# Layer 3 of a four-layer cross-attention kernel: a written plan of rounds for an item's four stages

## The chip, the core and the metric

The kernel runs on one core of a Trainium2 chip. The metric is the device time of one execution in microseconds (us); the time given for a kernel is the median of its runs. A profiled execution is a separate run, taken by the hardware profiler, with its own time.

## What is computed

The reference applies four transformer layers one after the other to `x` of 8 items of 256 tokens by 320 channels, in float32, with a context of 120 tokens by 192 channels per item. Layers 0 and 1 have self-attention, cross-attention and a gated feed-forward part, and layer 2 has cross-attention to the text and to the image tokens. The change is in layer 3, which has 8 heads of 40 channels:

```python
query = hidden_states @ Wq
keyt, valt = enc @ Wk, enc @ Wv                          # 116 context tokens
hs = _mha(query, keyt, valt)                             # 256 queries on 116 keys
ca_q1 = einsum('btc,th->bch', ca, Wq_ca)[:, indices, :]  # 192 distinct queries from 4 tokens
ca_hs1 = _mha(ca_q1, residual, residual)                 # 192 queries on the item's 256 tokens
ca_q2 = ca_hs1 @ Wq
ca_hs2 = _mha(ca_q2, ca @ Wk_ca, ca @ Wv_ca)             # on 4 keys
out = (hs + ca_hs2) @ Wout + b_out + residual
```

`_mha` is softmax attention. A softmax needs each query's largest score first, so every score is computed twice here: once to find the largest, once (with the largest already subtracted through an added row of the operands) for the exponential.

## The kernel before

TensorE multiplies into PSUM, which is cut into three double banks (`self.pair()`, tiles `pf`) and two single banks (`self.bank()`, tiles `pa`). A matmul that opens a new tile has to wait until the last reader of an earlier tile in that place is done. VectorE (DVE) finds maxima, takes reciprocals and normalises; ScalarE (ACT) takes exponentials and copies; GpSimd (POOL) adds the bias row; SyncE (SP) issues the DMAs.

`run_flow` goes over a list of 40 items; the last eight, one per batch entry, are layer 3's, built by `last_item`. Each item has four stages, written as generators, and each `yield` ends a step. In round `step` four generators are open together: the largest scores of the next item (`tops`), the projections of the item after that (`project`), the output product of the item before (`fin`), and the attention of the item itself (`out`). Before the change they advance in turn, one step each per turn, in that order, until all are empty. The Tile framework then sets each engine's fixed order of instructions from the order of emission, its priorities and its own estimates; on the chip every engine keeps to that order and waits on semaphores.

The steps of layer 3, with short names used in the rest of the text and the lines of the kernel before:

- **P1** transposes of the item (L339), loads of `cs`, `kz`, `v`, masks `bd` (L985). **P2** queries (lwq, L132 and L139). **P3** `z` and `u` (wz, L132, L139, L1009).
- **T1** largest scores of the queries: two halves of 16 matmul records (L1027), each with one maximum `negm` on DVE (L1031). **T2**, **T3** largest scores of the further attention (L1041, 16 records in two double banks), each with two maxima `negc` (L1046). **T4** transposes of these maxima (L1054, L1057), a copy to `nT` on ACT (L1061), and six small DMAs of `nT` into `cs` and `qT` (L1063, L1065).
- **O1** the further scores, first half, and exponentials (`further(0)`, L1077, L1083). **O2** nothing. **O3** `further(1)` and `further_values(0)` (L1109, reciprocal L1115, `oc` L1116). **O4** `context(0)` (L1092, exponential L1098) and `further_values(1)`. **O5** `context(2)`, the small softmax (product with `m` at L120, then `mx`, `p`, `sm`), `context_values(0)`. **O6** `context_values(1)` and `(2)`. **O7** `context_values(3)`, the product with `sel`, `pT`, `xb`. Each `context_values` is 16 records (L1123) into one single bank, a reciprocal `rs` (L1129) and a product `oT` (L1130) on DVE, which frees the bank.
- **F1**, **F2** one output product each (L120, 8 records with `lwo` and 2 with `v2W`), the addition to `x_sb` (L1185) and the store.

Of the kernel before, what the change touches and what calls it, by code (L numbers as in the profile page):

```python
# [54 lines left out]
class Kernel:  # L55
# [619 lines left out]
    def run_flow(self, items, before={}, after={}):  # L675


        n = len(items)
        made = {}
        for step in range(-2, n + 1):  # L680
            if step + 2 < n:
                if step + 2 in before:
                    before[step + 2]()
                made[step + 2] = items[step + 2]()
            order = ((step + 1, 1), (step + 2, 0), (step - 1, 3), (step, 2))
            gens = [made[i][k]() for i, k in order if 0 <= i < n]
            while gens:
                for g in list(gens):
                    try:
                        next(g)  # L690
                    except StopIteration:
                        gens.remove(g)
            if step in after:
                after[step]()

# [254 lines left out]
    def last_item(self, b, w, brow, to):  # L950
# [66 lines left out]
        def tops():  # L1017
            qT, kT, z, cs = it["q"], it["k"], it["z"], it["c"]
            negm = self.small.tile([P, 2, G3, TPB], F32, tag="negm", name="negm3")
            negc = self.small.tile([P, 4, 2, 2], F32, tag="negc", name="negc")  # L1020
            for g0 in range(0, G3, 2):
                s = self.pair()
                for i in range(2):
                    for t in range(TPB):
                        for j in range(2):
                            r, o = j * PAD3, (i * TPB + t) * K3
                            nc.tensor.matmul(  # L1027
                                s[:, j, o : o + K3], qT[r : r + PAD3, g0 + i, t * P : (t + 1) * P],
                                kT[r : r + PAD3, g0 + i, :], start=True, stop=True,
                            )  # L1030
                nc.vector.tensor_reduce(  # L1031
                    negm[:, :, g0 : g0 + 2, :].rearrange("p j g t -> p j (g t)"),
                    s[:, :, : 4 * K3].rearrange("p j (t k) -> p j t k", k=K3), AX.X, ALU.max, negate=True,
                )
            yield
            for g in range(2):
                s = [self.pair() for _ in range(2)]
                for t in range(2):
                    for j in range(4):
                        r = j * PAD  # L1040
                        nc.tensor.matmul(  # L1041
                            s[j // 2][:Q3, j % 2, t * N : (t + 1) * N], cs[r : r + PAD, g, t * Q3 : (t + 1) * Q3],
                            z[r : r + PAD, g, :], start=True, stop=True,
                        )
                for i in range(2):
                    nc.vector.tensor_reduce(  # L1046
                        negc[:Q3, 2 * i : 2 * i + 2, g, :], s[i][:Q3].rearrange("p j (t k) -> p j t k", k=N),
                        AX.X, ALU.max, negate=True,
                    )
                yield  # L1050
            nT = self.work.tile([8, 2 * N], F32, tag="nT", name="nT3", bufs=1)
            ps = self.bank()
            for t in range(2):
                nc.tensor.transpose(  # L1054
                    ps[:8, t * P : (t + 1) * P], negm.rearrange("p j g t -> p (j g) t")[:, :, t], self.ident
                )
                nc.tensor.transpose(  # L1057
                    ps[:8, N + t * Q3 : N + (t + 1) * Q3], negc[:Q3].rearrange("p j g t -> p (j g) t")[:, :, t],
                    self.ident[:Q3, :Q3],
                )  # L1060
            nc.scalar.copy(nT[:, : N + CC], ps[:8, : N + CC])  # L1061
            for g in range(2):
                nc.sync.dma_start(cs[T3::PAD, g, :], nT[g::2, N : N + CC])  # L1063
            for g in range(G3):
                nc.sync.dma_start(qT[D3::PAD3, g, :], nT[g::G3, :N])  # L1065
# [111 lines left out]
        def fin():  # L1177
            x, xb, (oT, pT) = self.x[:, TPB * b : TPB * (b + 1), :], it["xb"], it["out"]
            r = b * HT % P
            for t in range(TPB):  # L1180
# [5 lines left out]
                nc.sync.dma_start(to[b, o, :], x[:, t])  # L1186
                yield

        return project, tops, out, fin


class Quant:
# [630 lines left out]
```

## Time and profile before

| what | value |
|---|---|
| median of 3 runs | 2202.73 us (2201.51 to 2212.49) |
| profiled execution, its own time | 2203.86 us |
| its span, first to last instruction | 2202.1 us |
| TensorE (PE) busy | 2036.4 us, 92% of the span |
| VectorE (DVE) busy | 1112.6 us, 51% |
| ScalarE (ACT) busy | 833.3 us, 38% |
| layer 3's items, output product to output product | 34.92 us (2007.27 to 2042.19) |
| in such a stretch (2007 to 2042): PE, DVE, ACT busy | 33.54, 19.92, 9.62 us |

Line names such as L1129 are lines of the kernel before. A row of the timeline gives start, busy time, engine, line, operation and operands, a count, and the idle time ahead of it with what ended it. A busy PE row includes pipelined matmuls whose ends are modelled, so the start-to-start distance of two groups is the better cost of a group.

### The profile page before, as it was taken

Reading aid. Unit: us, or ns where it says so; the run is one execution under the profiler, and the core shown is the slowest. Engines: PE = TensorE matmul, PEld = TensorE weight load, DVE = VectorE, ACT = ScalarE, POOL = GpSimd, SP = SyncE. Lnnn points to the kernel's source line nnn. Section 1 sums busy time; section 2 is a strip of 40 time slices with the busy share of each in tenths; the row PEclk is TensorE's granted clock in tenths of the full one; section 3 lists DMA queues with packets and bytes.
Section 4 is the critical chain, followed back from the end, with each engine's and each line's share of the span. In section 5 each row is a group of like instructions: output and inputs, shape, how many; then the busy total and the mean of one; then the engine's idle time right before and its main releaser. Section 6 shows DMA issues by size and latency. Waiting matters only on the chain.

```text
span 2202.1 us, 38254 instructions
## 1 busy us (share of the span) xinstructions
PE 2036.4 (92%) x16415; PEld 1194.6 (54%) x16415; DVE 1112.6 (51%) x1698; ACT 833.3 (38%) x1259; POOL 330.5 (15%) x358
## 2 busy tenths in 40 slices
PE   7888889898889999999999998899999999999997
PEld 5643345554444465465555555544555655666664
DVE  5388687445651222235555567621121666546565
ACT  3456888367542121124444444311201333222221
POOL 3194033723010000000000010100000100000100
PEclk9989889898899999999999999999999999999999
DMA  4000000642120000020000101100000120000000
GB/s 118 20 12 2 2 1 1 174 111 57 52 85 14 1 0 1 1 93 2 2 2 22 28 25 36 47 1 0 1 0 1 24 68 23 19 16 26 23 19 16
DMA packets 79303, 63.21 MB, mean 29 GB/s; under 512 B 48410, under 2 KB 68318, under 8 KB 78622
## 3 DMA queue, kind: packets, MB, share of 16 engines
q1 hardware_dynamic: 75070, 57.06, 9.4%
q10 hardware_dynamic: 4064, 3.71, 0.6%
q8 instruction: 129, 2.11, 0.4%
q14 instruction: 40, 0.33, 0.0%
HBM read 42.61 MB, written 17.37 MB: 27 GB/s over the span
## 4 chain that ended last, share of the span: by engine, by line
PE 73%; DVE 15%; issue 4%; ACT 4%; POOL 2%; DMA 2%; SPq 0%; ACTq 0%; DVEq 0%; POOLq 0%
PE pf L594 13%; PE pf L120 11%; PE pf L132 9%; PE pa L120 7%; PE pa L456 6%; PE pf L439 4%; PE pa L594 3%; PE pf L139 3%; DVE negm L1456 3%; PE pf L394 3%; PE pf L736 3%; DVE rs L464 3%; PE pf L1497 2%; PE pa L1519 2%; DVE negm L401 2%
## 5 line engine op out<-in xcount | busy, mean ns | idle before, releaser
L445 ACT ACTIVATE e<-pf 128x1024 f32<-128x1024 f32 (+2 forms) x176 | 158.5, 946 | 220.1 <-PE pf L439 213.1
L401 DVE TENSOR_REDUCE negm<-pf 128x4 f32<-128x1024 f32 (+4 forms) x224 | 188.1, 887 | 97.9 <-PE pf L394 97.9
L594 PE MATMUL pf<-xTf,ff 128*128 128x512 f32 x512 | 230.8, 597 | 6.2 <-DVE negm L401 5.2
L464 DVE RECIPROCAL rs<-pa 128x256 f32<-128x256 f32 x88 | 152.3, 1745 | 143.5 <-PE pa L456 143.5
L1504 ACT ACTIVATE e<-pf,sc_s 128x1024 f32<-128x1024 f32 x160 | 169.8, 1118 | 48.7 <-PE pf L1497 44.8
L1456 DVE TENSOR_REDUCE negm<-pf 128x4 f32<-128x1024 f32 (+2 forms) x128 | 143.3, 1151 | 69.6 <-PE pf L1453 58.2
L619 DVE SCALAR_TENSOR_TENSOR hT<-pf,cols_sb,gl 128x512 f32<-128x512 f32 x64 | 48.0, 751 | 256.4 <-ACT gl L618 254.1
L120 PE MATMUL pf<-ff,hT 128*128 128x320 f32 x640 | 174.4, 434 | 0.0
L594 PEld LDWEIGHTS pf<-xTf,ff 128*128 128x128 f32 x512 | 94.3, 190 | 125.4 <-issue 118.5
L120 PEld LDWEIGHTS pf<-ff,hT 128*128 128x128 f32 x640 | 120.9, 190 | 55.5 <-issue 6.1
L618 ACT ACTIVATE gl<-pf,cols_sb 128x512 f32<-128x512 f32 x64 | 44.0, 689 | 247.8 <-PE pf L594 247.8
L439 PE MATMUL pf<-qT,kT 32*128 32x256 f32 (+1 forms) x1280 | 122.1, 410 | 9.1 <-DVE negm L401 7.5
L394 PE MATMUL pf<-kT,qT 32*128 32x120 f32 (+1 forms) x1920 | 113.1, 326 | 18.6 <-ACT e L445 18.3
L487 POOL TENSOR_TENSOR xb<-x_sb,brow 128x640 f32<-128x640 f32 x24 | 37.0, 1543 | 563.8 <-DVE x_sb L493 555.4
L120 PE MATMUL pa<-o,oT 128*128 128x320 f32 x352 | 105.7, 441 | 15.2 <-DVE oT L465 15.2
L394 PEld LDWEIGHTS pf<-kT,qT 32*128 32x128 f32 x1920 | 83.0, 186 | 58.4 <-ACT e L445 27.5
L647 POOL TENSOR_TENSOR xb<-x_sb,brow 128x640 f32<-128x640 f32 x16 | 25.0, 1563 | 573.8 <-DVE x_sb L652 528.2
L1497 PE MATMUL pf<-Q,K 32*128 32x256 bf16 (+1 forms) x960 | 90.5, 295 | 21.7 <-DVE negm L1456 11.5
L456 PE MATMUL pa<-e,v 128*32 128x256 f32 (+1 forms) x1280 | 106.1, 391 | 2.3 <-ACT e L445 1.7
L1606 DVE TENSOR_SCALAR w<-e 128x1024 bf16<-128x1024 f32 (+2 forms) x128 | 89.2, 703 | 32.3 <-ACT e L1504 31.1
L132 PE MATMUL pf<-xT,q 128*128 128x256 f32 x384 | 100.5, 391 | 0.4 <-ACT e L445 0.2
L439 PEld LDWEIGHTS pf<-qT,kT 32*128 32x128 f32 (+1 forms) x1280 | 68.4, 182 | 55.5 <-DVE negm L401 26.9
(291 smaller groups left out, 3439.2 us busy)
## 6 DMA issues: line engine op xcount, KB each, us to landing
ff<-in_L_xattn_Wff_dram SPq DMA_DIRECT2D x1, 2560.0 KB
qT<-nT SPq DMA_DIRECT2D x160, 4.0 KB
ff<-in_L_xattn_ff_w_dram SPq DMA_DIRECT2D x1, 2560.0 KB
out_dram<-x_sb SPq DMA_DIRECT2D x16, 160.0 KB
kd_cross<-kst SPq DMA_DIRECT2D x8, 300.0 KB
vd_cross<-vst SPq DMA_DIRECT2D x8, 300.0 KB
vd_both<-vst SPq DMA_DIRECT2D x8, 300.0 KB
kT<-kd_cross SPq DMA_DIRECT2D x8, 300.0 KB
```

Of the source, the lines that this page charges most:

```text
L120: self.nc.tensor.matmul(out, l, r, start=i == 0, stop=i == len(pairs) - 1)
L132: self.nc.tensor.matmul(o, *t[c], start=start and c == 0, stop=stop and c == n - 1, skip_group_check=True)
L394: nc.tensor.matmul(s[j // 2][:, j % 2, o : o + nk], qT[r : r + PAD, g, t * P : (t + 1) * P], kT[r : r + PAD, g, :nk], start=True, stop=True,)
L401: nc.vector.tensor_reduce(negm[:, n, 2 * i : 2 * i + 2, g0 : g0 + len(gs), :].rearrange("p j g t -> p j (g t)"), sv[:, :, :, k0:k1], AX.X, ...
L439: nc.tensor.matmul(s[j // 2][:ks, j % 2, o : o + N], kT[r : r + PAD, g, c * ks : (c + 1) * ks], qT[r : r + PAD, g, :], start=True, stop=True,)
L445: nc.scalar.activation(e[:ks, 2 * i : 2 * i + 2, :n], s[i][:ks, :, :n], AF.Exp, scale=scale)
L456: nc.tensor.matmul(o[j * PAD : (j + 1) * PAD, what * N : (what + 1) * N], w, es[g][:ks, j, c * N : (c + 1) * N], start=first and c == 0 an ...
L464: nc.vector.reciprocal(rs, o[:, N:])
L594: ins = nc.tensor.matmul(*args, **kw)
L1456: nc.vector.tensor_reduce(negm[:, 2 * h : 2 * h + 2, gs[0] : gs[-1] + 1, :].rearrange("p j g t -> p j (g t)"), s[:, :, : len(gs) * TPB * n ...
L1497: nc.tensor.matmul(s[at // 2][:ks, at % 2, o : o + N], l, m, start=not shift and o == 0, stop=shift and o + N == n, skip_group_check=True,)
L1504: nc.scalar.activation(e[:ks, :, :n], ps[:ks, :, :n], AF.Exp, scale=self.sc[:ks, 9:10])
```

## The change

The generators get letters: `t` for `tops`, `p` for `project`, `f` for `fin`, `o` for `out`. An item may carry a fifth element, a string. `run_flow` first advances the generators in the order of that string, one step per letter, and then lets what is left advance in turn as before. Items of other layers carry no string. `tops` also yields between the two halves of T1, for all layer 3 items, so it has five steps: T1a, T1b, T2, T3, T4.

```diff
+            order = {"t": (step + 1, 1), "p": (step + 2, 0), "f": (step - 1, 3), "o": (step, 2)}
+            gens = {n: made[i][k]() for n, (i, k) in order.items() if 0 <= i < n_items}
+            plan = made[step][4] if 0 <= step < n_items and len(made[step]) > 4 else ""
+            for what in plan.replace(" ", ""):
+                if what in gens:
+                    next(gens[what], None)
             while gens:
-                for g in list(gens):
+                for what in list(gens):
                     try:
-                        next(g)
+                        next(gens[what])
                     except StopIteration:
-                        gens.remove(g)
+                        del gens[what]
...
@@ tops
                 nc.vector.tensor_reduce(
                     negm[:, :, g0 : g0 + 2, :].rearrange("p j g t -> p j (g t)"),
...
-            yield
+                yield
             for g in range(2):
...
-        return project, tops, out, fin
+        return project, tops, out, fin, "pffoo po pot ot ot ot t"
```

The string gives a round of layer 3 the emission order P1 F1 F2 O1 O2, P2 O3, P3 O4 T1a, O5 T1b, O6 T2, O7 T3, T4. Before, it was T1 P1 F1 O1, T2 P2 F2 O2, T3 P3 O3, T4 O4, O5, O6, O7.

No instruction is added or taken away. What the two programs issue on PE in one full round of layer 3, from one O1 to the next, groups in order (T of the next item, P of the one after, F of the one before):

```
before: ... O1 with F1 between | T2 | P2 | F2 | T3 | P3 | further(1) | values f0 | T4 transposes | context 0
        values f1 | context 2 | m, 1 record pair of T1 inside | cv0 cv1 | T1a | cv2 | T1b | P1 | cv3 | sel
after:  O1 | P2 | further(1) | values f0 | P3 | context 0 | values f1 | T1a | context 2 | m | cv0 | T1b | cv1
        cv2 | T2 and 4 records of T3 | cv3 | sel | rest of T3 | 1 T4 transpose | P1 | 6 records of F1
        the other T4 transposes | rest of F1, F2
```

(cv0 to cv3 are the four `context_values`; two records of T2 stand ahead of cv2.) On DVE the round after the change has, from the small softmax on: sm, reciprocal cv0, the small reciprocal, oT cv0, the small product, negm, reciprocals cv1 and cv2, oT cv1 and cv2, negc, negc, reciprocal cv3, negc, oT cv3, negc, and then the two additions of F1 and F2. Before, both negm stood there and all four negc stood around the two additions. The orders of POOL are the same; on SP the six DMAs of `nT` now come right before the two stores of a round, and the loads of P1 after these.

More of the change, by code (lines that the diff above doesn't have):

```diff
@@ L675, in run_flow @@
     def run_flow(self, items, before={}, after={}):
-        n = len(items)
+        n_items = len(items)
         made = {}
-        for step in range(-2, n + 1):
-            if step + 2 < n:
+        for step in range(-2, n_items + 1):
+            if step + 2 < n_items:
                 if step + 2 in before:
@@ L684, in run_flow @@
                 made[step + 2] = items[step + 2]()
-            order = ((step + 1, 1), (step + 2, 0), (step - 1, 3), (step, 2))
-            gens = [made[i][k]() for i, k in order if 0 <= i < n]
+            order = {"t": (step + 1, 1), "p": (step + 2, 0), "f": (step - 1, 3), "o": (step, 2)}
[4 more added lines that the diff above has]
+                    next(gens[what], None)
             while gens:
-                for g in list(gens):
+                for what in list(gens):
                     try:
-                        next(g)
+                        next(gens[what])
                     except StopIteration:
-                        gens.remove(g)
+                        del gens[what]
             if step in after:
```

## The prediction

> **What bounds the kernel now.** I began with the page's sums (PE busy for 92% of the span) and then left them, since the change touches only the last 280 us. The busy times of a stretch as long as one item of layer 3 say what limits that stage:
>
> ```profile
> 2007.00:2042.00 35.00, 33.54 (x300) 22.84 (x299) 19.92 (x25) 9.62 (x15) 2.94 (x5) 1.00 0.08 25
> ```
>
> The columns are PE, weight loads, DVE, ACT, POOL, granted clock, DMA. PE has 1.5 us free of 35, at full clock; DVE is busy for 20. So a better order can win at most about 1.5 us per item, some 10 us in all. The waits of PE in that stretch are short:
>
> ```profile
> PE pa L1123 <- DVE oT L1130: 0.7, 1, 0.7
> PE pa L1123 <- DVE p L1158: 0.5, 1, 0.5
> ```
>
> These two, the longest, are waits of context_values for a single bank, and two such banks are all there are. DVE's timeline shows what they wait for:
>
> ```profile
> 2023.58 0.22 DVE L1155 TENSOR_REDUCE sm<-p 96x16 f32<-96x64 f32 x1 [0.32 <-ACT p L1153]
> 2023.81 1.76 DVE L1129 RECIPROCAL rs<-pa 128x256 f32<-128x256 f32 x1
> ...
> 2026.07 3.36 DVE L1129 RECIPROCAL rs<-pa 128x256 f32<-128x256 f32 x2
> 2029.35 0.68 DVE L1130 TENSOR_TENSOR oT<-pa,rs 128x256 f32<-128x256 f32 x2
> 2029.95 1.11 DVE L1031 TENSOR_REDUCE negm<-pf 128x8 f32<-128x928 f32 x1
> 2030.98 1.75 DVE L1129 RECIPROCAL rs<-pa 128x256 f32<-128x256 f32 x1
> 2032.65 1.06 DVE L1031 TENSOR_REDUCE negm<-pf 128x8 f32<-128x928 f32 x1
> 2033.63 0.41 DVE L1130 TENSOR_TENSOR oT<-pa,rs 128x256 f32<-128x256 f32 x1
> 2036.37 0.49 DVE L1185 TENSOR_TENSOR x_sb<-pa,xb 128x320 f32<-128x320 f32 x1 [2.34 <-PE pa L120]
> ```
>
> From sm (2023.58) to the last oT (2034.04) DVE does not pause: over the values it, not PE, sets the pace, for 10.5 us, and after it there is slack (2.34 us). The chain that ended last agrees: it is on PE outside this piece and on DVE inside it.
>
> **The change, part by part.** No instruction is added, so every cost is one of order.
>
> *What moves on DVE.* All four negc used to stand behind the values, by the output products. Now three stand ahead of the last oT and the fourth right behind it. One negm leaves the stretch (T1a's maximum is now ahead of mx). DVE from sm to the last oT, by start-to-start distances of rows above: sm to the second reciprocal 2023.58 to 2026.07 = 2.49; one negm 1.03; two reciprocals 3.28; two oT 0.60; two negc 2.35 (the pair L1046 at 2036.79); reciprocal 1.67; negc 1.17; oT 0.41. Sum 13.0 us, against 10.5.
>
> *What PE has to fill it with.* Set sm at 0. PE ended the m product at about -0.8. Then cv0 1.08, T1b 1.15, cv1 1.08 end at 2.5; cv2 needs the bank of cv0, free at 2.44 + 0.14 = 2.6, and ends near 3.7; ten matmuls of T2 and T3 end near 5.0. cv3 needs the bank of cv1, freed by the first oT of the pair: 2.49 + 1.03 + 3.28 + 0.30 + 0.14 = 7.2. So PE waits about 2.3 us, where before it waited 0.7. Then cv3 1.04, sel 0.98, the rest of T3 1.0, one transpose and P1 1.0 end near 11.3; F1 needs a bank too, and both are taken: one by T4 (held until all four negc are done and nT is copied), one by cv3 until 13.0 + 0.14. A second wait, of 1.8 us.
>
> *The cycle of one item.* From the first product of F1 all else is PE without a wait, by distances of the chain in order of time:
>
> ```profile
> 2012.94 0.63 PE pf L139 x4
> 2013.57 1.26 PE pf L1009 x12
> 2014.83 0.86 PE pf L1077 x16
> 2015.69 1.44 PE pa L1109 x32
> ...
> 2017.62 1.05 PE pf L1092 x8
> 2018.67 1.48 PE pa L1109 x32
> ...
> 2166.44 6.16 PE pa L120 x20
> ```
>
> F1 and F2 6.16, T4's transposes 0.49, O1 0.86, P2 1.92 + 1.06 + 1.92 = 4.90, further(1) 0.86, values 1.44, P3 1.92 + 0.63 + 1.26 = 3.81, context 1.05, values 1.48, T1a 1.15, context 1.05, m 0.90: 24.15. From m to sm 0.82 (2022.76 to 2023.58), DVE 13.0, one hop 0.14. Sum 38.1 us, against 34.9 to 35.2 now: **3.1 us more per item**, because one loop now runs through PE's 24 us and DVE's 13 us one after the other.
>
> *The whole.* Between the products of items 0 and 5 (1972.35 to 2143.51) the trace has 171.2 us; five cycles are 190.5: +19.3. The last two items: item 6 has no projections beside it, 8.8 of PE + 0.8 + 13.0 + 6.65 + hops = about 30, against 26.0 now; item 7 has O1 and further(1) (1.7, and 0.8 for their banks) behind the products of item 6 instead of ahead: together +6.5. The start: by item 0's products less work is done than before (a P2 4.90, one T1 2.2, one O1 and further(1) 1.7, half a T2 1.05), and the two new waits stand there (+2.4): -7.5. Sum +18.3.
>
> *The clock.* The trace shows what a wait can cost besides itself. Windows of 3.4 us with their successors:
>
> ```profile
> 962.70:966.10 3.40, 1.61 (x14) 1.15 (x18) 3.37 (x6) 3.26 (x5) 1.28 (x2) 1.00 1.00 343
> 966.10:969.50 3.40, 3.40 (x33) 2.59 (x26) 1.40 (x2) 1.94 (x2) 0.00 (x0) 0.51 0.34 116
> 874.00:877.40 3.40, 2.03 (x5) 1.06 (x6) 3.15 (x5) 1.56 (x4) 0.86 (x2) 1.00 0.02 5
> 877.40:880.80 3.40, 2.74 (x20) 1.10 (x18) 0.62 (x1) 0.00 (x0) 0.00 (x0) 1.00 0.00 0
> 1211.90:1215.30 3.40, 1.91 (x17) 0.99 (x16) 2.35 (x3) 1.69 (x4) 0.00 (x0) 1.00 0.00 0
> 1215.30:1218.70 3.40, 3.40 (x34) 1.38 (x32) 0.00 (x0) 1.78 (x2) 0.00 (x0) 0.50 0.00 0
> ```
>
> With 1.61 or 1.91 us busy the next stretch is granted half the clock; with 2.03 it is not. A wait of 2.3 us leaves a window that idle unless the window's edge cuts it about in the middle, so I expect it in most of seven rounds. Its price lies between 0 (the slow work falls into the second wait) and 3.4 us (two windows, none covered); I take 0.6, near the lower end, since 1.8 us of waiting follow at once: +4. All: +22, which on the median is 2225; I forecast 2222, a little less, as the stretches of PE were taken at their widest.
>
> The Trainium skill's page "TensorE: Matmul & The Clock Gate" (section "Why this matters for your kernels") speaks for a cheaper outcome: it asks only that gaps stay below about 3 us for the clock to hold. By that the sum is +18, or 2221; the windows above differ from it, since one with 1.8 us free and one with 1.5 were followed by half the clock, and I go by them.
>
> *With no cost.* T4's DMAs: nT is copied 0.66 us after T4, and O1 reads cs behind the rest of the products (4.3 us), so a DMA has 3.6 us to land; no row shows its landing, and before there were 12 us for it, so the bound is 0 to 1.5 us per round; I take 0. On SP the stores queue behind the six DMAs, each issue about 0.5 us, and nobody waits for a store; the loads of P1 have most of a round. POOL's order is unchanged. In rounds of layer 2 only the first layer 3 item's tops are cut finer, in a stage where PE has work at every step: 0.
>
> **The rivals.** *Faster*: T2 and T3 fill PE's waits and DVE keeps up; PE then runs free at 33.5 us per item, 1.5 less, six to seven times: about -10, 2193. It decides at the point where DVE's stretch is below about 9.9 us, that is, where the three negc (4.7 with the fourth) don't stand ahead of the last oT. The page's PE share of 92% speaks for it; DVE's list speaks against it. *No change*: the waits only move, as the 1.5 us that PE now loses are given back elsewhere: 2195 to 2212. Against it: cv3's new wait alone is longer than today's two together. *Dearer*: every round also loses two clock windows in which PE's work is on the path, 7 x 2.5 more, or T4's DMAs are late as well: 2232 to 2250. *The plan has no effect*, because the scheduler reorders anyway: no, the issued orders differ as described.
>
> **How the numbers follow.** The run that was profiled took 2203.86 us, 1.1 above the median, and the difference is set on the median 2202.73: main case 2222, its own range 2212 to 2231 (chance 0.7). Dearer 0.16. No change 0.1. Faster 0.04. Half a per cent, 11 us, is about what a measurement of this kernel can tell from no change (its three runs span that). Slower by more: 0.85, the main and the dearer case less a little at the lower edge; same 0.11; faster 0.04. The range that should hold 8 in 10 reaches from 2207 to 2242.
>
> **What would show it.** Right: in layer 3's full rounds one product to the next takes 37 to 39 us; DVE from sm to the last oT 13 us without a pause; PE waits near 2.3 us before a context_values for oT L1134 (its new line), and near 1.8 us before the first lwo product, for the same; granted clock below 1.00 in some windows after 1945. Wrong: rounds at 35 us or below; waits on PE below 1 us; or a wait of O1 (L1081) for a DMA as the longest, which I priced at nothing. If rounds are at 38 us but the total is not +15 or more, my account of the first and last rounds fails.

## The result and the profile after

| | before | after |
|---|---|---|
| median of 5 runs each, beside each other | 2201.76 us (2201.51 to 2212.49) | 2227.76 us (2213.42 to 2233.89) |
| profiled execution, its span | 2203.86 us, 2202.1 us | 2219.95 us, 2218.2 us |
| mean granted clock of the profiled execution | 0.971 | 0.966 |

The ratio is 1.0101, with a 95% interval of 1.0072 to 1.013: slower by 1%, some 22 us, inside the range. The changed kernel's runs differ by 20 us, and the difference follows the granted clock: 2213.42 us at a mean granted clock of 0.971, 2219.95 at 0.966, 2233.89 at 0.957.

The timeline of DVE in a full round of layer 3, from the small softmax to the first addition (start, busy time, instruction; in brackets the idle time ahead of it):

```profile
2021.11 0.21 DVE L1159 TENSOR_REDUCE sm<-p 96x16 f32<-96x64 f32 x1 [0.32 <-ACT p L1157]
2021.29 1.76 DVE L1133 RECIPROCAL rs<-pa 128x256 f32<-128x256 f32 x1
...
2023.56 1.11 DVE L1035 TENSOR_REDUCE negm<-pf 128x8 f32<-128x928 f32 x1
2024.59 3.35 DVE L1133 RECIPROCAL rs<-pa 128x256 f32<-128x256 f32 x2
2027.87 0.68 DVE L1134 TENSOR_TENSOR oT<-pa,rs 128x256 f32<-128x256 f32 x2
2028.47 2.34 DVE L1050 TENSOR_REDUCE negc<-pf 96x4 f32<-96x1024 f32 x2
2030.74 1.74 DVE L1133 RECIPROCAL rs<-pa 128x256 f32<-128x256 f32 x1
2032.43 1.22 DVE L1050 TENSOR_REDUCE negc<-pf 96x4 f32<-96x1024 f32 x1
2033.57 0.41 DVE L1134 TENSOR_TENSOR oT<-pa,rs 128x256 f32<-128x256 f32 x1
2033.90 1.21 DVE L1050 TENSOR_REDUCE negc<-pf 96x4 f32<-96x1024 f32 x1
2038.91 0.49 DVE L1189 TENSOR_TENSOR x_sb<-pa,xb 128x320 f32<-128x320 f32 x1 [3.80 <-PE pa L120]
```

From sm to the end of the last oT it works without a pause for 12.9 us (2021.11 to 2033.98), where it took 10.5. Three negc stand ahead of the last oT. PE's waits, first in the round from 2116 to 2154, then in the one from 2002.6 to 2041.2 (total, number, longest):

```profile
PE pa L1127 <- DVE oT L1134: 2.0, 1, 2.0
PE pa L120 <- DVE oT L1134: 1.1, 1, 1.1
```

```profile
PE pa L1127 <- DVE oT L1134: 2.0, 1, 2.0
```

The first line is cv3 waiting for a bank, the second the first output product F1. In the earlier of the two rounds F1's wait is missing. The clock shows why. That whole round first, then stretches of 3.4 us around its wait (length; busy time of PE, weight loads, DVE, ACT and POOL, with the number of instructions; granted clock; DMA share and GB/s):

```profile
2002.60:2041.20 38.60, 36.64 (x302) 24.04 (x304) 19.80 (x25) 9.47 (x15) 2.99 (x5) 0.91 0.07 23
...
2026.10:2029.50 3.40, 1.44 (x11) 0.69 (x10) 3.40 (x5) 0.00 (x0) 0.00 (x0) 1.00 0.00 0
2029.50:2032.90 3.40, 3.40 (x16) 1.35 (x15) 3.40 (x4) 0.36 (x1) 0.00 (x0) 0.50 0.20 62
2032.90:2036.30 3.40, 3.40 (x13) 2.50 (x12) 2.21 (x3) 1.21 (x3) 0.00 (x0) 0.50 0.02 8
2036.30:2039.70 3.40, 3.40 (x15) 1.92 (x14) 0.49 (x1) 0.52 (x1) 0.00 (x0) 1.00 0.00 1
```

The stretch with the wait has 1.44 us of work; the next two are granted half the clock, and PE, working slowly, reaches the output product when its bank is already free. In layer 3 the clock is at half in seven places while PE works: one each in the second to the sixth full round and one in each of the last two items (before: one, in the last item). Four of the five full rounds have it right behind cv3's wait. The other, with its sm at 1982.21, has it behind F1's wait of 1.7 us, so that F1 itself runs at half the clock:

```profile
1991.90:1995.30 3.40, 1.71 (x20) 1.06 (x13) 3.40 (x5) 1.25 (x4) 0.00 (x0) 1.00 0.15 55
1995.30:1998.70 3.40, 3.40 (x9) 1.88 (x9) 0.81 (x1) 0.00 (x0) 0.00 (x0) 0.51 0.00 0
```

The chain that ended last runs through DVE alone from sm to the output product in the first two rounds, as the forecast had it. In a later round it leaves DVE after the first oT of the pair, goes through cv3 and T3 to a negc, and then back to PE:

```profile
2137.41 1.10 DVE negm L1035
2138.51 3.28 DVE rs L1133 x2
2141.79 0.29 DVE oT L1134
2142.08 0.14 issue
2142.21 1.97 PE pa L1127 x8
2144.18 1.66 PE pa L120 x4
2145.85 0.66 PE pf L1045 x8
2146.51 0.02 issue
2146.53 1.22 DVE negc L1050
2147.75 0.34 DVE oT L1134
2148.09 0.14 issue
2148.23 1.85 PE pa L120 x6
```

cv3 ran here at half the clock (1.97 us; 1.02 us from its start to that of the product with sel where the clock was full, at 1989.47) and pushed T3's third negc and the last oT back.

### The profile page after: what moved, and what is told of

The parts are those of the page before. It is cut to its first block, busy times and chain, and to the rows that moved or that the text cites. A ratio compares the mean times of both kernels' runs of the same rounds, so it can differ in the third digit from the quotient of the medians.

```text
span 2218.2 us, 38278 instructions
## 1 busy us (share of the span) xinstructions
PE 2046.7 (92%) x16415; PEld 1197.3 (54%) x16415; DVE 1107.9 (50%) x1698; ACT 831.5 (37%) x1259; POOL 329.3 (15%) x358
## 4 chain that ended last, share of the span: by engine, by line
PE 71%; DVE 16%; issue 4%; ACT 4%; POOL 2%; DMA 1%; SPq 0%; ACTq 0%; DVEq 0%; POOLq 0%
PE pf L594 13%; PE pf L120 11%; PE pf L132 9%; PE pa L120 7%; PE pa L456 6%; PE pf L439 4%; PE pa L594 3%; PE pf L139 3%; DVE negm L1462 3%; PE pf L394 3%; DVE rs L464 3%; PE pf L740 2%; PE pa L1525 2%; PE pf L1503 2%; DVE negm L401 2%
## 5 line engine op out<-in xcount | busy, mean ns | idle before, releaser
L1612 DVE TENSOR_SCALAR w<-e 128x1024 bf16<-128x1024 f32 (+2 forms) x128 | 88.5, 697 | 33.5 <-ACT e L1510 32.0
```

## The experiments

The time of a whole kernel also moves with the clock granted in layers 0 to 2 (in the profiled executions 0.97 up to 1900 us for the kernels before and after, 0.96 for the one with 20 more products), so each experiment is read twice: by its ratio to the kernel before, run beside it, and by one full round of layer 3 in its trace, from the third item's sm to the fourth's. Line numbers shift a little from kernel to kernel, with the lines that an edit adds.

| kernel | round, us | sm to end of last oT, us | median, us | ratio to before, 95% interval |
|---|---|---|---|---|
| before | 34.9 | 10.5 | | |
| after | 38.6 (later ones 37.6) | 12.9 | 2227.76 | 1.0101, 1.0072 to 1.013 |
| cut alone | 35.6 | 9.9 | 2202.98 | 1.0022, 1.0001 to 1.0042 |
| string alone | 43.8 | 13.0 | 2248.35 | 1.0238, 1.0209 to 1.0266 |
| string alone, filled | 40.6 (first and fifth 37.7) | 13.0 | 2228.90 | 1.0132, 1.009 to 1.0174 |
| after, half maxima | 38.5 (37.1 to 40.1) | 12.3 (10.9 to 13.3) | 2213.82 | 1.0077, 1.0044 to 1.0111 |
| after, 32 more products | 38.4 | 13.9 | 2228.17 | 1.0143, 1.0101 to 1.0185 |
| after, 20 more products | 37.2 | 12.8 | 2221.62 | 1.0097, 1.0064 to 1.013 |
| half maxima and 20 more | 36.0 | 11.1 | 2208.22 | 1.0022, 1.0009 to 1.0036 |
| string A | 33.4 | 11.9 | 2201.52 | 1.0011, 0.9994 to 1.0028 |
| string B | 33.9 (to 34.2) | 10.5 | 2201.78 | 1.0000, 0.9984 to 1.0015 |
| string C | 33.9 | 17.4 | 2199.77 | 0.9997, 0.9981 to 1.0013 |
| string A, first six items | 33.4 | 11.9 | 2194.67 | 0.9969, 0.9944 to 0.9994 |
| the same, last item filled | 33.4 | 11.9 | 2190.57 | 0.9951, 0.9927 to 0.9974 |

**Which half of the change costs.** The cut of T1 alone:

```diff
-        return project, tops, out, fin, "pffoo po pot ot ot ot t"
+        return project, tops, out, fin
```

> The cut of T1 alone, without the string: the generators advance in turn as before. Theory (the string's order puts three negc ahead of the last oT, and the loss is DVE's stretch): here DVE from sm to the last oT is as before, one negm and no negc, 10.5 us; PE waits below 1 us; rounds of 35 to 36 us; time 2200 to 2209, clock windows at 0.50 in layer 3 as before (one place). Rival (the finer cut of T1 is what costs, as it moves maxima among the values): 2215 to 2230, rounds of 37 us or more.

The string alone:

```diff
                 nc.vector.tensor_reduce(negm[...], ...)
-                yield
+            yield
```

> The string alone, T1 in one step: every letter t then comes one step earlier, T2 beside context_values 0. Theory: four negc and no negm stand from sm to the last oT, 2.49 + 2.35 + 3.28 + 0.60 + 2.35 + 1.67 + 0.41 = 13.2 us; the wait before cv3 grows by the second negc, 1.2 to 1.4 us, to 3.5 to 4 us, and the one before the output product shrinks; rounds 37.5 to 39 us, time 2220 to 2238, several windows at half clock. Rival (the cut makes the loss): 2200 to 2210.

The cut alone gives rounds of 35.6 us and 0.2% more time: at most a small part of the loss. The string makes it, as the theory had it, but the size was wrong: 43.8 us a round and 2248 us, where 37.5 to 39 and at most 2238 were expected from DVE's stretch, which is 13.0 (expected 13.2). The next round, of 44.0 us (2079.8 to 2123.8), shows where the 5 us above the expected 39 may have gone, and its waits what may have started it:

```profile
2079.80:2123.80 44.00, 37.99 (x302) 24.12 (x304) 19.77 (x26) 9.47 (x15) 2.98 (x5) 0.84 0.07 20
```

```profile
PE pa L1127 <- DVE oT L1134: 3.2, 1, 3.2
PE pa L1058 <- ACT pT L1175: 1.7, 1, 1.7
```

The clock is granted at 0.84 on average: 13.7 us of the round run at half. This was tested in the string alone by filling the wait with work that nobody reads:

```diff
+                if g == 1:
+                    for k in range(28):
+                        j, r = k % 4, k % 4 * PAD
+                        nc.tensor.matmul(s[j // 2][Q3:, j % 2, :N], cs[r : r + PAD, 0, :PAD],
+                                         z[r : r + PAD, 0, :], start=True, stop=True)
                 for i in range(2):
                     nc.vector.tensor_reduce(negc[...], ...)
```

> The string without the cut of T1 (rounds of 43.8 us, 13.7 us of each at half the clock, where 38 were expected) with 28 matmuls more, 3.1 us, behind T3, in the wait of 3.6 us before cv3 (they write partitions of T3's banks that nobody reads). Theory (the 5 us above the expected round are the clock alone: a wait of 3.6 us starts it, the slow work makes the next waits): clock 1.00 through the full rounds, DVE's stretch still 13.0, rounds 37 to 39 us, time 2210 to 2225. Rival (the other order makes the round, through T4 and its copy ahead of the output product, and the clock only follows): rounds 42 us or more.

Neither side is right throughout, and the time, 2228.90 us, is above the 2225 of the theory. In the first and fifth round the clock held and the round took 37.7 us: nothing of the excess is left. In the three between them one stretch of 3.4 us stayed at half, and the round took 40.6. The windows around the output product, a slow round first, then the fifth:

```profile
2045.10:2048.50 3.40, 1.42 (x10) 0.79 (x8) 2.02 (x2) 2.09 (x5) 0.00 (x0) 1.00 0.15 58
2048.50:2051.90 3.40, 3.40 (x8) 1.76 (x6) 0.00 (x0) 0.00 (x0) 0.00 (x0) 0.50 0.02 4
...
2126.90:2130.30 3.40, 2.44 (x10) 1.45 (x9) 1.34 (x2) 1.34 (x4) 0.00 (x0) 1.00 0.12 42
2130.30:2133.70 3.40, 3.40 (x18) 2.03 (x18) 0.49 (x1) 0.00 (x0) 0.00 (x0) 1.00 0.14 50
```

With 1.42 us of work in the stretch before it, the output product (F1) runs at half the clock, and nothing follows that could take this up: about 1.7 of the 2.9 us. The rest, 1.2 us, is a later start (13.85 us after sm, in the fifth round 12.65): T4 waits for the copy pT (1.3 us) in the slow rounds and not in the fifth. ACT's order makes that wait. In the slow rounds pT stands behind two copies xT of P1, in the first and fifth ahead of them (a slow round, then the fifth):

```profile
2045.98 0.36 ACT L343 COPY xT<-pf 64x256 f32<-64x256 f32 x1
2046.37 0.36 ACT L1182 COPY pT<-pa 32x256 f32<-32x256 f32 x1
...
2125.82 0.36 ACT L1182 COPY pT<-pa 32x256 f32<-32x256 f32 x1 [10.57 <-PE pa L120]
```

In the string alone one to three of these copies stand ahead of pT in every full round, and its waits above hold 1.7 us for pT. So the order has a part in the excess, which the theory left out. The rounds at 37.7 differ in both the clock and ACT's order, so how much each costs in the string alone is not shown.

**Is DVE's stretch the round's length?** The maxima negc over half of their columns:

```diff
-                        negc[:Q3, 2 * i : 2 * i + 2, g, :], s[i][:Q3].rearrange("p j (t k) -> p j t k", k=N),
+                        negc[:Q3, 2 * i : 2 * i + 2, g, :],
+                        s[i][:Q3].rearrange("p j (t k) -> p j t k", k=N)[:, :, :, : N // 2],
```

> The changed kernel, with each negc maximum taken over half of its columns (it leaves out the other half of the further scores in the maximum); PE's order is nearly the same. Theory: a negc takes 0.6 instead of 1.15 us, DVE from sm to the last oT falls from 12.9 to about 11.2, the wait before cv3 stays at 2.3 to 2.5 (no negc lies ahead of it), the wait before the first output product falls from 2.0 to 0.3; rounds fall by 1.5 to 1.7 us to 36 to 36.5, time 2213 to 2219. Rival (PE's own order and its banks make the loss, DVE's length does not count): rounds as in the changed kernel, 37.5 to 38.9, time 2222 to 2230.

The total fits the theory (2213.82 us), the rounds, expected at 36 to 36.5, do not: after a first one of 40.1 they alternate between 37.1 and 38.5 us. DVE now has pauses that it did not have:

```profile
2077.80 1.76 DVE L1134 RECIPROCAL rs<-pa 128x256 f32<-128x256 f32 x1 [0.50 <-PE pa L1128]
2080.29 0.69 DVE L1050 TENSOR_REDUCE negc<-pf 96x4 f32<-96x512 f32 x1 [0.73 <-PE pf L1045]
```

cv3 and T3 are late, at half the clock, after the wait of 2.0 us that remained. So the clock had to be taken out of the question first, with 32 products more ahead of cv3 (the edit shown above, at g == 0):

> The changed kernel with 32 matmuls more per item (96 to 127 of the partitions of T2's banks, read by nobody) that stand between T2 and T3, about 2.3 us, in the wait before cv3. Theory of the clock (a wait of 2.5 us leaves a stretch of 3.4 us with under 2 us of work, and the next is granted half the clock): the wait before cv3 falls below 0.5 us, DVE's stretch and the rounds without half clock stay at 37.5, but the half-clock stretches in layer 3 fall from eight places to at most three, and the time falls by 5 to 13 us to 2214 to 2222 with a smaller spread. Rival (the half clock has nothing to do with PE's waits): eight places as before, 2224 to 2230 or more.

From the first sm to the sixth the clock stayed at 1.00, so PE's wait is what takes it away. The time did not fall (2228.17 us, expected 2214 to 2222): 32 products took 3.6 us, not 2.3, negc waited 1.1 us for them, DVE's stretch grew to 13.9 and the round to 38.4. With 20 (2.3 us):

> The changed kernel with 20 matmuls more per item in T2's banks (partitions 96 to 127, read by nobody), 2.2 us instead of the 3.6 of the longer filling, so that negc no longer waits for them. Theory (the round is DVE's stretch of 12.9 us behind PE's 24, and half the clock costs little because a second wait takes it up): DVE from sm to the last oT 12.9 without a pause, clock 1.00 through the full rounds, rounds 37.3 to 37.7 us, so 0.3 to 0.6 below the changed kernel's 38.0, time 2215 to 2227. Rival (the half clock is worth 2 us or more per round): rounds of 36 us or less.

```profile
2056.30:2093.50 37.20, 35.95 (x345) 23.36 (x341) 19.69 (x25) 9.46 (x15) 3.00 (x5) 1.00 0.08 24
```

Rounds of 37.2 us at full clock, with DVE's stretch as in the changed kernel's rounds at full clock (12.8). That is a little more gain than the expected 0.3 to 0.6 us. It is the round without the clock's part; the slow clock adds 0.4 to 1.7 us to it. The changed kernel's own first full round, the only one without slow clock, agrees: 37.2 us from sm to sm (1945.0 to 1982.2). Both together:

> The same filling together with negc maxima over half of the columns (leaves out the other half of the further scores in the maximum). With half maxima alone a negc took 0.6 us, but cv3 ran at half the clock and DVE paused 0.9 to 1.2 us for it, so rounds fell by only 0.3 to 0.9. Theory (DVE's stretch is the round's length, the slow clock hid it): stretch 11.2 to 11.4 us, rounds 35.6 to 36.2, time 2203 to 2214. Rival (PE's own order limits to 37 us): 37 us or more.

The stretch falls from 12.8 to 11.1 us and the round from 37.2 to 36.0; 1.7 us off DVE give 1.2 off the round. By then PE is busy for 35.91 of 36.0 us, the additional products included, and is the bound again:

```profile
2042.90:2078.90 36.00, 35.91 (x342) 23.31 (x342) 17.80 (x25) 9.47 (x15) 2.99 (x5) 1.00 0.08 25
```

So, at full clock, DVE's stretch sets the changed kernel's round.

**Does a long stretch have to cost?** Three other strings, which put the projections P2 and P3 among the values. A:

```diff
-        return project, tops, out, fin, "pffoo po pot ot ot ot t"
+        return project, tops, out, fin, "ffotototopotopopt"
```

> Another string, 'ffotototopotopopt': F1 F2 O1, then T1, T2 and T3 spread among O2 to O4, the projections late, so that the 12 lwq products of P2 stand between cv2 and cv3 and those of P3 behind sel. On DVE two negc stand from sm to the last oT, about 11.7 us. Theory (what costs is that PE has nothing to do beside DVE's stretch, not the stretch's length): PE has 4 to 5 us of work there and runs without a wait above 0.7 us, rounds fall to PE's own 33.5 to 34.5 us, time 2188 to 2200, no half clock beside layer 3's last rounds. Rival (any negc in the stretch costs its length): rounds 36 to 37 us, 2205 to 2215.

B, "ffootototopopopot":

> String 'ffootototopopopot': as the other one, but T2 and T3 so placed that no negc and no negm stands ahead of the last oT; DVE from sm to the last oT about 9.5 us. P1 and P2 stand among the values. Theory: rounds 34 to 34.5 us, 2188 to 2200. Rival (the length of DVE's stretch alone counts): rounds below those of the other string by 2 us.

C, "offotootpoptoptot":

> String 'offotootpoptoptot': all four negc from sm to the last oT, as many as in the changed kernel or more, about 13.2 us, but P2's queries and P3 stand on PE between the values. Theory (PE's work beside the stretch decides): rounds 34 to 35 us, time 2192 to 2204, waits before cv3 below 1 us. Rival (DVE's stretch with its negc decides): rounds 38 us, time 2220 to 2230, as in the changed kernel.

C decides it. Its DVE stretch is the longest of all, 17.4 us (about 13.3 of work), with all four negc in it and two pauses that wait for PE:

```profile
2054.62 2.35 DVE L1050 TENSOR_REDUCE negc<-pf 96x4 f32<-96x1024 f32 x2 [3.60 <-PE pf L1045]
2056.90 3.35 DVE L1133 RECIPROCAL rs<-pa 128x256 f32<-128x256 f32 x2
...
2061.36 2.35 DVE L1050 TENSOR_REDUCE negc<-pf 96x4 f32<-96x1024 f32 x2 [0.51 <-PE pf L1045]
```

Its round is 33.9 us all the same, and the longest wait on PE in it is 0.7 us, for the copy nT. B, with no negc in the stretch, is not better than A with two (33.9 to 34.2 against 33.4). The length of DVE's stretch costs nothing where PE has work beside it: the changed kernel does P2 and P3 ahead of the values and has only T2 and T3 left, and these need DVE themselves.

The times missed the expectation for A and B (2201.52 and 2201.78, expected 2188 to 2200): rounds 0.7 to 1.5 us shorter than the third round before, but no gain in all. The last two items give it back. From the sixth output product (its last record, here and below) to the end A takes 67.5 us, before 56.0: with no projection left, its order waits 4.9 us for one bank, and 13.7 us near the end run at half the clock. From P1 of the first layer 3 item to the end A takes 338.5 us and before 340.9. So A for the first six items, and the old turns for the rest:

```diff
-        return project, tops, out, fin, "pffoo po pot ot ot ot t"
+        return project, tops, out, fin, "ffotototopotopopt" if b < 6 else ""
```

> The string 'ffotototopotopopt' for the first six items and none for the last two, whose stages advance in turn. In full rounds the string took 33.4 us against 34.9 to 36.3 before; its last two items lost this again (33.4 + 29.7 + 24.6 us from the sixth sm to the end against 27.6 + 22.0 + 22.5). Theory (the loss of that string lies in the last two items, where no projection stands beside the values): a gain of 2 to 6 us on the string for all items, 2193 to 2199. Rival (the last items' loss is only work that the string put later): no gain, 2199 to 2204.

The same with 17 products more in the last item; `spare(n)`, a helper that is not shown, issues n products of kT and qT into a double bank that nobody reads, for the last item (`b == 7`) alone:

```diff
             context_values(1)
+            spare(7)
             context_values(2)
             yield
+            spare(10)
             context_values(3)
```

> As the last one, with 17 matmuls more in the last item (into a double bank that nobody reads): 7 between context_values 1 and 2, 10 between 2 and 3, where PE waited 2.1 and 3.2 us and was granted half the clock for the 13.7 us up to the last output product. Theory (those waits cost the clock at the end, where all of PE's work is on the path): no half clock in the last 15 us, 2 to 5 us less than without the filling, 2189 to 2197. Rival (the clock is lost anyway, or the work there is not limited by it): within 1 us of the other.

From the sixth output product to the end: 58.1 us, and 53.4 with the additional products; from P1 of the first item to the end 334.3 and 329.7. A stretch of 10.2 us in the last item, without them and with them (two traces; it begins 5.5 and 3.6 us after sm):

```profile
2170.50:2180.70 10.20, 8.96 (x21) 4.41 (x22) 3.15 (x5) 0.36 (x1) 0.00 (x0) 0.50 0.00 0
```

```profile
2170.50:2180.70 10.20, 9.74 (x52) 5.76 (x50) 5.84 (x7) 0.36 (x1) 0.00 (x0) 1.00 0.05 18
```

At full clock it takes 18.1 instead of 22.8 us from the last item's sm to the end. By the whole time the two cannot be told apart (their intervals overlap, the medians differ by 4.1 us); by the traces they can. Both are ahead of the kernel before by half a per cent or less, with intervals below 1: the ratios are 0.9969 and 0.9951.

## Why the prediction was right, step by step

**The mechanism.** Nearly all that was to be seen is there: DVE 12.9 us without a pause (forecast 13.0), a wait of cv3 for the bank that the pair's oT frees (2.0 us in the list of waits; forecast 2.3), stretches at half the clock. The wait of the first output product has its size (1.7 us; forecast 1.8) only in the two rounds where the clock was full up to it; in the other four it is 1.1, 0.5, 0.5 and none, as slow work ahead of it took its place, which is what the forecast priced the slow clock by. No wait of O1 for a DMA appears among PE's waits in the full rounds: nothing was the right price.

**The sum**, by the two profiled executions. P1 of the first layer 3 item to its output product went from 113.5 to 107.6 us: -5.9 (forecast -7.5). From there to the sixth product 171.4 became 190.3: +18.9 (forecast +19.3, without the clock). From there to the end 56.0 became 64.0: +8.0 (forecast +6.5). The products are taken by the last record of each item. The measured pieces hold the slow clock, the forecast ones do not. Together +21.0, against +22 with the clock. The profiled executions differ by only 16.1, since the later one was 4.9 us ahead at that P1, before anything of the changed rounds; the medians differ by 26.0.

**Several terms were off, and cancel; that the sum came within 1 us is in part luck.** A cycle without the clock's part is 37.2 us, by the kernel with 20 more products, not 38.1. DVE's part was right (12.8 of 13.0); PE's 24.15 us from the first output product to the end of m measure 23.4. F2 and O1 overlap by 0.4, T1a, the context after it and m take 2.7 instead of 3.1. The text said that these were taken at their widest; that was worth 0.8 us per round, some 4 us in five cycles, where the forecast had taken off 3 in all. Against this stand the start, which won 1.6 us less than forecast, the last two items, which lost 1.5 more (their slow clock included), and the clock. The clock was priced at 0.6 us per round and took 0.8 on average in the five cycles (38.06 against 37.2), by the way that was named: part of the slow work falls into the second wait. What the sum did not see is that the slow clock also delays cv3 and T3, and these DVE's last steps.

**The rivals.** *Faster* was to be decided by DVE's stretch, below 9.9 us. The experiments show that to be the wrong point: string C is at 33.9 us a round with 17.4. What decides is PE's own work beside the stretch. The floor that the rival named, 33.5 us a round, was right: string A reached 33.4. *Dearer* named two slow windows a round on the path and 2232 to 2250 us. The string alone came to that time (2248 us), with up to five slow windows a round and the later copy pT; the changed kernel differs from it by the cut of T1 alone, and so the cut spared it this.

**The skill's rule.** The Trainium skill's page "TensorE: Matmul & The Clock Gate", section "Why this matters for your kernels", lets gaps below about 3 us pass. Here waits of 2.0 us (four rounds) and 1.7 us (one) were followed by half the clock in five of six full rounds, and with the first of them filled the clock stayed at 1.00. The measurement decides against the rule for this case. The total could not have told them apart (2222 against 2221); the windows do.

## What to carry to other kernels

When an order is changed, ask what the bounding engine has to do while the other engine works through its chain, and not how long that chain is: put work between its steps that needs nothing from it. Price a wait of the bounding engine with the clock that it can cost, and look at what stands right after it: slow work that falls into another wait cost 0.4 us a round here, and an output product run slowly on the path 1.7. An order that is best in the full rounds may be the wrong one for the last items, where the filling work has run out.

## What the runs showed of the hardware

A wait of PE of 2.0 us (four rounds) or 1.7 us (one) was followed by half the clock for the next 3.4 or 6.8 us in five of six full rounds; with cv3's wait filled by 20 products this was gone. The stretch of 3.4 us ahead of the slow one held 1.44 to 1.71 us of work. In the first full round the same two waits lay across the edges of such stretches, with 2.79, 2.15 and 1.82 us of work in them, and the clock stayed. Since 1.91 was once followed by half the clock (the forecast's window at 1211.90), there is no sharp bound between them. Products that nobody reads kept it up: 17 of them made the last item 4.7 us shorter.

The time of a run follows its mean granted clock closely: 14 runs of the kernel before went from 2191.35 us at 0.978 to 2204.01 us at 0.970, about 1.6 us for each thousandth, and five of the changed kernel from 2213.42 at 0.971 to 2233.89 at 0.957, about 1.5. The profiled executions of strings A to C had a mean clock of 0.966 to 0.968 where the kernel before, beside them, had 0.972. Their traces put this mostly behind 1900 us: up to there they are granted 0.97 as before, behind it A and B 0.96, C 0.97 and before 0.98. A's last two items have 20.5 us at half the clock, those of before 10.2.
